# An edge layer's sum over pairs, laid out with four pair members of 32 channels in the partitions

## The chip, the cores and the metric

The kernel runs on one core of a Trainium2 chip, alone. The metric is the device time in microseconds of one execution; a lower number is better. The profile is one execution taken by the hardware profiler. It names the engines PE (TensorE matmul), PEld (TensorE weight load), DVE (VectorE), ACT (ScalarE), POOL (GpSimd) and SP (SyncE, which here only issues DMAs).

## What is computed

The reference applies four residual layers to an image batch of shape (4, 56, 56, 128): a window and global attention layer, an edge layer, a Fourier layer and a convolution. The change is in the second one:

```python
# x: (4, 56, 56, 128), after a group norm
W1, W2 = (We[:, :f], We[:, f:])
proj_i = jnp.einsum('blnf,of->blno', x, W1)
proj_j = jnp.einsum('blnf,of->blno', x, W2)
edge = jax.nn.relu(proj_i[:, :, :, None, :] + proj_j[:, :, None, :, :] + be)
edge_sum = edge.sum(axis=3)
node_in = jnp.concatenate([x, edge_sum], axis=-1)
node = jax.nn.relu(jnp.einsum('blnc,oc->blno', node_in, Wn) + bn)
```

For each image b, each line l of 56 and each channel o of 128, all 56 x 56 pairs (n, m) are formed, and their relu is summed over m. That is 4 x 56 x 56 x 56 x 128 relus, about 90 million, and no matrix product can replace them. The relu of a sum can be written without an addition: relu(a + c) = max(a, -c) + c. So an engine may take one maximum per pair, and the sum of c over those m is put in afterwards as a correction that depends on l alone.

## The kernel before

Channels lie in the 128 partitions, and an image's 3136 positions lie along the free dimension. The program is one instruction stream per engine. In `build` (L2689) four images go one after another through `first_layers`: an attention stage (`fast_layer`), then `edge_layer` (L1150), then a store of x1. The next image's attention stage starts with memsets on POOL (L339 and on), which wait until the buffers of the edge layer are released.

`edge_layer` works in seven blocks j of 8 lines (NB = 448 positions). For each block:

- `normed(j)` makes the group-normed input xg, for the first two blocks on DVE, then on ACT (L1178).
- `project(j)` (L1180) multiplies xg by W2 and W1 into two PSUM tiles, pc and pa (L1184, L1186).
- `evacuate(j)` (L1189) copies c = -(pc + be) and a = pa to SBUF on ACT (L1194, L1196), and adds the bias bn to the residual x (L1197). GpSimd works from SBUF; DVE reads a from PSUM, as pa.
- Fourteen turns take four m each, in the order of `EDGE_TURNS` (L1147). In a `d` turn DVE writes max(a, c) for four m and all 448 positions, 1792 elements per partition, into a tile e_td (L1231; seven buffers). In a `p` turn POOL writes a - c into e_tp (L1233; four buffers), and ACT takes the relu in place (L1235).
- After each turn PE adds the tile to the accumulator acc in PSUM (L1238). A turn is sixteen matmuls with a 32x32 identity: row group r is a quarter of the channels, column group q one of the four m. acc is four banks, one for each channel quarter, and the four m stay apart in its partition quarters.
- `rest` is the sum of c over the m of the `d` turns (DVE, L1248). e_sums is acc copied to SBUF (ACT, L1250).
- `output(j, rest, sums)` (L1200) adds up six matmuls of 128x128x448: xg by Wn, the correction by rest (L1203), and one for each channel quarter of the sums (L1206), whose weights Wnq sum the four m at the same time.
- `finish(j, po)` (L1209) is one DVE operation: x = max(po, -bn) + x.

The order is written out by hand for PE, ACT and DVE. At the end of block j PE does the output of block j - 1 and the projections of block j + 2; DVE does the `finish` of block j - 2 after turn 3 of block j; ACT evacuates block j + 1 after turn 5. [...] two for pc and po (tag mm), two for pa, four for acc.

After the fourth image, `build` (L2775 to L2788) loads images back from memory into a pool x2 of two buffers, s_x, for the Fourier layer. SP issues these loads in its queue as soon as the memory of the buffers is free, and then stores x1 (x2d) and loads that layer's weights (t_w_qk and others). The first matmuls of that layer read s_x (L1527).

Of the kernel before, what the change touches and what calls it, by code (L numbers as in the profile page):

```python
# [12 lines left out]
F32 = mybir.dt.float32  # L13
AF = mybir.ActivationFunctionType
ALU = mybir.AluOpType
AX = mybir.AxisListType
PSUM = bass.MemoryType.PSUM
DRAM = bass.MemoryType.DRAM

P = 128  # L20
B = 4
HH = 56
TOK = HH * HH
NB = 448
# [8 lines left out]
def bc(ap, axis, n):  # L33

    ap = ap.unsqueeze(axis)
    shape = list(ap.shape)
    shape[axis] = n
    return ap.to_broadcast(shape)


def blk(j):
    return slice(j * NB, (j + 1) * NB)
# [149 lines left out]
def apply_norm(k, out, xt, mr):  # L192
    k.nc.vector.tensor_scalar(out, xt, mr[:, 0:1], mr[:, 1:2], ALU.subtract, ALU.mult)
# [950 lines left out]

EDGE_TURNS = "ddpddpdpddpddp"  # L1147


def edge_layer(k, w, x1, st):  # L1150

    nc, tc = k.nc, k.tc
    xf = x1.rearrange("p l n -> p (l n)")
    nd = 4 * EDGE_TURNS.count("d")
    quarters = [slice(32 * q, 32 * q + 32) for q in range(4)]
    with ExitStack() as es:  # L1160
        big = es.enter_context(tc.tile_pool(name="e_big", bufs=1))
        wk = es.enter_context(tc.tile_pool(name="e_wk", bufs=2))
        psum = es.enter_context(tc.tile_pool(name="e_ps", bufs=2, space=PSUM))

        def bank():
            return psum.tile([P, 512], F32, tag="mm", name="e_mm")

        mr = group_norm_factors(k, wk, bank, st)
        xg = big.tile([P, TOK], F32, name="e_xg")
        shift = wk.tile([P, 1], F32, name="e_shift", bufs=1)  # L1170
        nc.vector.tensor_scalar(shift, mr[:, 0:1], mr[:, 1:2], -1.0, ALU.mult, ALU.mult)
        ready = {}

        def normed(j):
            if j < 2:
                apply_norm(k, xg[:, blk(j)], xf[:, blk(j)], mr)
            elif j < NBLK:
                nc.scalar.activation(xg[:, blk(j)], xf[:, blk(j)], AF.Identity, bias=shift, scale=mr[:, 1:2])  # L1178

        def project(j):  # L1180
            if j >= NBLK:
                return
            pc = psum.tile([P, 512], F32, tag="mm", name="e_pc")
            nc.tensor.matmul(pc[:, :NB], w.W2, xg[:, blk(j)], start=True, stop=True)  # L1184
            pa = psum.tile([P, 512], F32, tag="pa", name="e_pa")
            nc.tensor.matmul(pa[:, :NB], w.W1, xg[:, blk(j)], start=True, stop=True)  # L1186
            ready[j] = pa, pc

        def evacuate(j):  # L1189
            if j >= NBLK:  # L1190
                return
            pa, pc = ready[j]
            c = wk.tile([P, 8, HH], F32, name="e_c")
            nc.scalar.activation(c.rearrange("p l m -> p (l m)"), pc[:, :NB], AF.Identity, bias=w.nbe, scale=-1.0)  # L1194
            a = wk.tile([P, NB], F32, name="e_a")
            nc.scalar.copy(a, pa[:, :NB])  # L1196
            nc.scalar.activation(xf[:, blk(j)], xf[:, blk(j)], AF.Identity, bias=w.bn)  # L1197
            ready[j] = pa, a, c

        def output(j, rest, sums):  # L1200
            po = psum.tile([P, 512], F32, tag="mm", name="e_po")
            nc.tensor.matmul(po[:, :NB], w.Wn[:, 0, :], xg[:, blk(j)], start=True, stop=False)
            nc.tensor.matmul(po[:, :NB].rearrange("p (l n) -> p l n", l=8), w.nWn, bc(rest, 2, HH),  # L1203
                             start=False, stop=False)
            for r in range(4):
                nc.tensor.matmul(po[:, :NB], w.Wnq[:, r, :], sums[:, r, :], start=False, stop=(r == 3))  # L1206
            return po

        def finish(j, po):  # L1209

            nc.vector.scalar_tensor_tensor(xf[:, blk(j)], po[:, :NB], w.nbn, xf[:, blk(j)], ALU.max, ALU.add)

        with tc.manual_schedule(engines={mybir.EngineType.PE, mybir.EngineType.Activation, mybir.EngineType.DVE}):
            for j in range(2):
                normed(j)
            for j in range(2):
                project(j)
                evacuate(j)
            last = po = None
            for j in range(NBLK):  # L1220
                pa, a, c = ready.pop(j)
                acc = psum.tile([P, 4, 512], F32, name="e_acc", bufs=1)
                rest = wk.tile([P, 8], F32, name="e_rest")
                at = {"d": 0, "p": nd}
                for g, e in enumerate(EDGE_TURNS):
                    t = wk.tile([P, 4, 8, HH], F32, tag="e_" + e, name="e_t" + e, bufs=7 if e == "d" else 4)
                    cm = bc(c[:, :, at[e]:at[e] + 4].rearrange("p l m -> p m l"), 3, HH)
                    at[e] += 4
                    if e == "d":
                        am = bc(pa[:, :NB].rearrange("p (l n) -> p l n", l=8), 1, 4)  # L1230
                        nc.vector.tensor_tensor(t, am, cm, ALU.max)  # L1231
                    else:
                        nc.gpsimd.tensor_sub(t, bc(a.rearrange("p (l n) -> p l n", l=8), 1, 4), cm)  # L1233
                        tf = t.rearrange("p m l n -> p (m l n)")
                        nc.scalar.activation(tf, tf, AF.Relu)  # L1235
                    for q in range(4):
                        for r, o in enumerate(quarters):
                            nc.tensor.matmul(acc[quarters[q], r, :NB], k.ident[o, o],  # L1238
                                             t[o, q].rearrange("p l n -> p (l n)"),
                                             start=(g == 0), stop=(g == len(EDGE_TURNS) - 1))  # L1240
                    if g == 3 and po is not None:
                        finish(j - 2, po)
                    if g == 5 and j:
                        evacuate(j + 1)
                    if g == 8:
                        normed(j + 2)
                    if g == 9:
                        nc.vector.tensor_reduce(rest, c[:, :, 0:nd], AX.X, ALU.add)  # L1248
                sums = wk.tile([P, 4, NB], F32, name="e_sums")
                nc.scalar.copy(sums, acc[:, :, :NB])  # L1250
                if last:
                    po = output(*last)
                project(j + 2)
                last = j, rest, sums
            finish(NBLK - 2, po)
            finish(NBLK - 1, output(*last))


def edge_weights(k, w, pool):

    for n, t in (("nbe", w.be), ("nbn", w.bn), ("nWn", w.Wn[:, 1, :])):
        r = pool.tile(list(t.shape), F32, name="e_" + n)
        k.nc.vector.tensor_scalar_mul(r, t, -1.0)
        setattr(w, n, r)


def l1_host(i):
    We, Wn = i["L1_conv_We"], i["L1_conv_Wn"]
    W2 = Wn[:, P:].T.reshape(4, 1, 32, P)
    return {  # L1270
        "w1_W1": We[:, :P].T, "w1_W2": We[:, P:].T, "w1_be": i["L1_conv_be"].reshape(P, 1),
        "w1_Wn": Wn.T.reshape(2, P, P).transpose(1, 0, 2), "w1_bn": i["L1_conv_bn"].reshape(P, 1),
        "w1_Wnq": np.broadcast_to(W2, (4, 4, 32, P)).reshape(4, P, P).transpose(1, 0, 2),
    }


# [1388 lines left out]
def group_norm_factors(k, pool, bank, st):  # L2665

    nc = k.nc
    mv = pool.tile([P, 2], F32, tag="mv", name="gf_mv")
    nc.vector.bn_aggr(mv, st.rearrange("p a b -> p (a b)"))
    ps = bank()  # L2670
    nc.tensor.matmul(ps[:, 0:1], k.g4, mv[:, 0:1], start=True, stop=True)
    mr = pool.tile([P, 2], F32, tag="mr", name="gf_mr")
    nc.vector.tensor_copy(mr[:, 0:1], ps[:, 0:1])
    t = pool.tile([P, 1], F32, tag="gt", name="gf_t")
    nc.vector.tensor_sub(t, mv[:, 0:1], mr[:, 0:1])
    nc.vector.tensor_mul(t, t, t)
    nc.vector.tensor_add(t, t, mv[:, 1:2])
    ps = bank()
    nc.tensor.matmul(ps[:, 0:1], k.g4, t, start=True, stop=True)
    nc.scalar.activation(t, ps[:, 0:1], AF.Sqrt, bias=k.eps)  # L2680
    nc.vector.reciprocal(mr[:, 1:2], t)
    return mr
# [158 lines left out]
```

## Time and profile before

| what | us |
|---|---|
| median of three runs | 3583.2 |
| lowest and highest | 3579.53, 3584.5 |
| the profiled execution, its own time | 3579.81 |
| its span, from first to last instruction | 3578.0 |
| mean granted TensorE clock | 0.981 |
| edge layer of the first image: first e_xg to last `finish` | 549.24 to 699.71 |
| edge layer of the fourth image: the same | 2540.12 to 2690.83 |
| DVE busy with e_td (L1231), whole program | 491.2 |
| POOL busy with e_tp (L1233), whole program | 451.5 |
| PE busy with e_acc (L1238), whole program | 548.4 |

The shares on the page's first line are means over the whole program: the edge layer is about 600 of 3578 us, so a share over the program says little about what bounds it. The table by stretches is of more use: it gives each engine's busy time within a given stretch. The operations of one kind are grouped by line and shape, with the number, the busy time in all, the mean of one, and the idle time of the engine just before them with what ended it. Operations of one engine overlap a little, so the distance between two of them is less than the mean of one. The ends of matmuls are modelled, and a matmul of fp32 stands as two records.

### The profile page before, as it was taken

The page shows a single profiled execution, that of the slowest core. Times are in us where ns is not written, and L with a number is a line of the kernel's source. Part 1 is how long each engine was busy: PE and PEld are TensorE (multiplying, and loading weights), DVE is VectorE, ACT ScalarE, POOL GpSimd, SP SyncE. Part 2 cuts the span into 40 slices and gives each one's busy share as a digit, 9 for nine tenths or more (in the row PEclk, how much of TensorE's full clock was granted, in tenths as well). Part 3 has the DMA queues.
Part 4 walks back from the last instruction along what each step waited for, and adds up shares of the span by engine and source line. Part 5 has one row for each costly group of instructions (what it writes and reads, how often), then busy time and mean ns, then how long its engine had stood idle before and what let it go on. Part 6 is the DMA issues. An engine that isn't in the chain of part 4 may idle for free.

```text
span 3578.0 us, 80873 instructions
## 1 busy us (share of the span) xinstructions
PE 3372.0 (94%) x36096; PEld 1549.4 (43%) x36096; DVE 2702.3 (76%) x2531; ACT 2089.9 (58%) x2103; POOL 1249.2 (35%) x752
## 2 busy tenths in 40 slices
PE   6999998989999898999999999999898899999998
PEld 4433344553333455333344643333456443336664
DVE  6588868767888696688859758887784678886776
ACT  4688865458888564688856458887552112214442
POOL 1000017600000581000018400000673778884686
PEclk8999999999999999999999999999998999999999
DMA  2144420014333000444310024442103027763101
GB/s 103 43 92 92 95 42 20 20 47 94 88 88 83 20 3 20 99 93 94 89 44 3 20 57 94 94 94 63 38 3 101 15 53 178 181 148 91 55 19 55
DMA packets 98076, 244.51 MB, mean 68 GB/s; under 512 B 64456, under 2 KB 69832, under 8 KB 92712
## 3 DMA queue, kind: packets, MB, share of 16 engines
q0 software_dynamic: 16128, 102.77, 14.2%
q1 hardware_dynamic: 74872, 123.64, 11.9%
q10 hardware_dynamic: 6720, 12.85, 1.3%
q8 instruction: 285, 4.67, 0.5%
q14 instruction: 71, 0.58, 0.1%
HBM read 79.46 MB, written 31.33 MB: 31 GB/s over the span
## 4 chain that ended last, share of the span: by engine, by line
PE 79%; DVE 10%; ACT 4%; issue 4%; POOL 3%; DMA 0%; POOLq 0%; DVEq 0%; ACTq 0%
PE f_pm L818 17%; PE f_pm L684 15%; PE u_po L1878 8%; PE e_acc L1238 7%; PE q_acc L1732 3%; DVE e_td L1231 3%; PE f_pm L791 2%; PE e_po L1206 2%; PE f_pm L770 2%; ACT f_ring L821 1%; PE f_pm L464 1%; PE o_d L2141 1%; DVE f_acc L673 1%; PE o_d L2538 1%; PE f_pm L715 1%
## 5 line engine op out<-in xcount | busy, mean ns | idle before, releaser
L821 ACT ACTIVATE f_ring<-f_pm 128x1792 f32<-128x1792 f32 (+1 forms) x764 | 1093.8, 1482 | 228.7 <-PE f_pm L818 181.2
L673 DVE TENSOR_TENSOR f_acc<-f_acc,f_ring 128x1792 f32<-128x1792 f32 x468 | 947.7, 2025 | 191.1 <-ACT f_ring L821 160.9
L818 PE MATMUL f_pm<-f_qT,f_kT 32*128 32x448 f32 x5376 | 725.2, 571 | 15.5 <-ACT f_ring L821 5.1
L684 PE MATMUL f_pm<-f_ring,f_va 128*32 128x448 f32 (+1 forms) x6304 | 589.4, 490 | 0.0
L663 POOL DMA_DIRECT2D f_far<-f_ring x112 | 96.6, 862 | 1329.3 <-ACT f_ring L821 1108.2
L1231 DVE TENSOR_TENSOR e_td<-e_pa,e_c 128x1792 f32<-128x1792 f32 x252 | 491.2, 2018 | 14.1 <-ACT e_a L1196 14.1
L1233 POOL TENSOR_TENSOR e_tp<-e_a,e_c 128x1792 f32<-128x1792 f32 x140 | 451.5, 3261 | 101.4 <-PE e_acc L1238 59.8
L818 PEld LDWEIGHTS f_pm<-f_qT,f_kT 32*128 32x128 f32 x5376 | 260.4, 183 | 417.2 <-ACT f_ring L821 304.7
L1238 PE MATMUL e_acc<-e_td,t_shared 32*32 32x448 f32 x8064 | 325.8, 545 | 24.9 <-DVE e_td L1231 24.0
L684 PEld LDWEIGHTS f_pm<-f_ring,f_va 128*32 128x32 f32 x6304 | 164.2, 109 | 409.7 <-issue 397.4
L1873 DVE TENSOR_TENSOR u_ud<-u_px,u_d 112x1792 f32<-112x1792 f32 x144 | 263.5, 1864 | 39.6 <-PE u_po L1878 35.4
L1235 ACT ACTIVATE e_tp<-e_tp 128x1792 f32<-128x1792 f32 x140 | 233.4, 1694 | 74.0 <-POOL e_tp L1233 74.0
L1875 POOL TENSOR_TENSOR u_up<-xh,u_d 112x1792 f32<-112x1792 f32 (+1 forms) x72 | 240.9, 3376 | 55.0 <-PE u_po L1878 39.7
L1238 PE MATMUL e_acc<-e_tp,t_shared 32*32 32x448 f32 x4480 | 222.6, 544 | 3.0 <-ACT e_tp L1235 2.4
L1878 PE MATMUL u_po<-u_ud,AT 112*64 112x448 f32 x1056 | 213.8, 544 | 1.9 <-DVE u_ud L1873 1.9
L1238 PEld LDWEIGHTS e_acc<-e_td,t_shared 32*32 32x32 f32 x8064 | 142.3, 103 | 138.4 <-DVE e_td L1231 79.4
L1878 PEld LDWEIGHTS u_po<-u_ud,AT 112*64 112x64 f32 x1056 | 74.4, 138 | 128.8 <-issue 112.9
L1250 ACT COPY e_sums<-e_acc 128x1792 f32<-128x1792 f32 x28 | 46.3, 1652 | 136.2 <-PE e_acc L1238 136.2
L1238 PEld LDWEIGHTS e_acc<-e_tp,t_shared 32*32 32x32 f32 x4480 | 96.5, 103 | 53.0 <-issue 16.6
L728 DVE RECIPROCAL f_den<-f_den 128x448 f32<-128x448 f32 x28 | 82.6, 2951 | 44.1 <-ACT f_den L725 44.1
L1717 POOL TENSOR_TENSOR q_u<-iS,q_g 128x1792 f32<-128x1792 f32 x32 | 102.8, 3236 | 23.0 <-PE q_acc L1732 22.8
L1732 PE MATMUL q_acc<-q_u,S 64*64 64x448 f32 x1024 | 104.6, 553 | 4.4 <-DVE q_u L1719 3.3
(525 smaller groups left out, 4511.6 us busy)
## 6 DMA issues: line engine op xcount, KB each, us to landing
f_far<-f_ring POOLq DMA_DIRECT2D x112, 896.0 KB, 6.3
u_d<-dd SPq DMA_DIRECT2D x46, 784.0 KB
f_far<-f_ring SPq DMA_DIRECT2D x28, 896.0 KB
xw<-in_x SPq DMA_DIRECT2D x4, 1568.0 KB
x2d<-x SPq DMA_DIRECT2D x4, 1568.0 KB
xat<-x SPq DMA_DIRECT2D x4, 1568.0 KB
x_xs<-xat ACTq DMA_DIRECT2D x32, 196.0 KB
xm<-x_ev ACTq DMA_DIRECT2D x64, 98.0 KB
```

Source lines behind the costliest of these rows:

```text
L673: nc.vector.tensor_add(e.acc, e.acc, slots(j, c))
L684: nc.tensor.matmul(e.po[heads[h], part], va[o, c, heads[h]], p, start=(c == 0), stop=(c == 23 and part.stop == NB))
L818: nc.tensor.matmul(ss[:, i, :NB], kT[heads[h], c * P:(c + 1) * P], qT[heads[h], blk(j)], start=True, stop=True)
L821: nc.scalar.activation(ring[:, slot:slot + m, :], ss[:, :m, :NB], AF.Exp, scale=scale)
L1231: nc.vector.tensor_tensor(t, am, cm, ALU.max)
L1233: nc.gpsimd.tensor_sub(t, bc(a.rearrange("p (l n) -> p l n", l=8), 1, 4), cm)
L1235: nc.scalar.activation(tf, tf, AF.Relu)
L1238: nc.tensor.matmul(acc[quarters[q], r, :NB], k.ident[o, o], t[o, q].rearrange("p l n -> p (l n)"), start=(g == 0), stop=(g == len(EDGE_TUR ...
L1732: nc.tensor.matmul(acc[bp][i][halves[hb % 2], hb // 2, :NB], x[o], u[o, 8 * hb:8 * hb + 8, :].rearrange("p h t -> p (h t)"), start=first, ...
L1873: nc.vector.tensor_mul(u, bc(px[:, :, :NB], 2, m), dm)
L1875: nc.gpsimd.tensor_mul(u, bc(x, 2, m), dm)
L1878: nc.tensor.matmul(po[64 * b2:64 * b2 + 64, :NB], st.AT[:, 8 * i + h0 + q, 2 * bp + b2, :], u[:, b2, q, :], start=(left == 16), stop=(left ...
```

## The change

The layout of a turn is turned round. Before, a turn has four m in the free dimension and 128 channels in the partitions. Now a turn has four m, one from each quarter of the 56, in the four partition quarters, with 32 channels in each, and the four channel quarters r lie in the free dimension.

- `l1_host` lays W1 out so that each channel quarter r has its own 128x128 weight that repeats 32 channels four times; be is laid out the same way. `project` makes four pa tiles of 448 columns, and one pc from sixteen small matmuls (32 output partitions, 112 columns) with -W2.
- `evacuate` copies the four a to SBUF with the bias be, and c; it is split into two parts, after turns 5 and 8.
- `terms` forms a turn. On DVE the first operand is a in SBUF, the second is pc in PSUM; on POOL it is a and c in SBUF.
- A turn of PE is four matmuls with 128 rows and 32 output partitions. The weight S sums the four m. acc is one bank, and its four quarters are the channel quarters, so the sums are 128x448 instead of 128x1792.
- The correction by rest is added into acc with -S, and `output` has two matmuls instead of six.
- Of fourteen turns eight are `d`, five `p`, and one `s`, half on DVE and half on POOL (before: nine and five). e_td has six buffers, and the half tiles have two buffers each. The banks of PSUM: one for po, four for pa, two for pc, one for acc.
- In block 0 the first three `d` turns and the first `p` turn are made quarter by quarter, as the a tiles arrive.

```diff
-EDGE_TURNS = "ddpddpdpddpddp"
+EDGE_TURNS = "ddpddpsdpdpddp"
...
-            pc = psum.tile([P, 512], F32, tag="mm", name="e_pc")
-            nc.tensor.matmul(pc[:, :NB], w.W2, xg[:, blk(j)], start=True, stop=True)
-            pa = psum.tile([P, 512], F32, tag="pa", name="e_pa")
-            nc.tensor.matmul(pa[:, :NB], w.W1, xg[:, blk(j)], start=True, stop=True)
+            pa = [psum.tile([P, 512], F32, name="e_pa", bufs=4) for r in range(4)]
+            pc = psum.tile([P, 512], F32, name="e_pc", bufs=2)
+
+            def first(r):
+                nc.tensor.matmul(pa[r][:, :NB], w.W1[:, r, :], xg[:, blk(j)], start=True, stop=True)
+            first(0)
+            xm = xg[:, blk(j)].rearrange("p (l m) -> p l m", l=8)
+            for r, o in enumerate(quarters):
+                for q in range(4):
+                    nc.tensor.matmul(pc[quarters[q], 8 * M * r:8 * M * (r + 1)].rearrange("p (l m) -> p l m", l=8),
+                                     w.nW2[:, o], xm[:, :, M * q:M * (q + 1)], start=True, stop=True)
+            for r in range(1, 4):
+                first(r)
...
+            for r in range(2 * part, 2 * part + 2):
+                nc.scalar.activation(a[:, r, :], pa[r][:, :NB], AF.Identity, bias=w.be[:, r:r + 1])
+                if r == 0:
+                    nc.scalar.copy(c.rearrange("p r l m -> p (r l m)"), pc[:, :NB])
+            if part == 1:
+                nc.scalar.activation(xf[:, blk(j)], xf[:, blk(j)], AF.Identity, bias=w.bn)
+
+        def terms(j, m, t, r0, r1, e):
+
+            pc, _, c, a = ready[j]
+            if e == "d":
+                c = pc[:, :NB].rearrange("p (r l m) -> p r l m", r=4, l=8)
+            cm = bc(c[:, r0:r1, :, m], 3, HH)
+            am = a[:, r0:r1, :].rearrange("p r (l n) -> p r l n", l=8)
+            if e == "d":
+                nc.vector.tensor_tensor(t, am, cm, ALU.max)
+            else:
+                nc.gpsimd.tensor_sub(t, am, cm)
+                tf = t.rearrange("p r l n -> p (r l n)")
+                nc.scalar.activation(tf, tf, AF.Relu)
...
-            nc.tensor.matmul(po[:, :NB].rearrange("p (l n) -> p l n", l=8), w.nWn, bc(rest, 2, HH),
-                             start=False, stop=False)
-            for r in range(4):
-                nc.tensor.matmul(po[:, :NB], w.Wnq[:, r, :], sums[:, r, :], start=False, stop=(r == 3))
+            nc.tensor.matmul(po[:, :NB], w.Wn[:, 1, :], sums, start=False, stop=True)
...
-                acc = psum.tile([P, 4, 512], F32, name="e_acc", bufs=1)
-                rest = wk.tile([P, 8], F32, name="e_rest")
-                at = {"d": 0, "p": nd}
+                acc = psum.tile([P, 512], F32, name="e_acc")
+                rest = wk.tile([P, 4, 8], F32, name="e_rest")
+                at, ms = {"d": 0, "p": nd + ns, "s": nd}, []
...
-                    for q in range(4):
-                        for r, o in enumerate(quarters):
-                            nc.tensor.matmul(acc[quarters[q], r, :NB], k.ident[o, o],
-                                             t[o, q].rearrange("p l n -> p (l n)"),
-                                             start=(g == 0), stop=(g == len(EDGE_TURNS) - 1))
+                    elif e == "s":
+                        parts = [(tile_of("d", 2), 0), (tile_of("p", 2), 2)]
+                        for t, r in parts:
+                            terms(j, m, t, r, r + 2, "p" if r else "d")
+                    else:
+                        parts = [(tile_of(e), 0)]
+                        terms(j, m, parts[0][0], 0, 4, e)
+                    for t, r0 in parts:
+                        for r in range(t.shape[1]):
+                            nc.tensor.matmul(acc[quarters[r0 + r], :NB], w.S[:, 0, :], t[:, r].rearrange("p l n -> p (l n)"),
+                                             start=(g == 0), stop=False)
...
-                sums = wk.tile([P, 4, NB], F32, name="e_sums")
-                nc.scalar.copy(sums, acc[:, :, :NB])
+                for r in range(4):
+                    nc.tensor.matmul(acc[quarters[r], :NB].rearrange("p (l n) -> p l n", l=8), w.S[:, 1, :],
+                                     bc(rest[:, r, :], 2, HH), start=False, stop=True)
+                sums = wk.tile([P, NB], F32, name="e_sums")
+                nc.scalar.copy(sums, acc[:, :NB])
```

More of the change, by code (lines that the diff above doesn't have):

```diff
@@ L1157, in edge_layer @@
     xf = x1.rearrange("p l n -> p (l n)")
-    nd = 4 * EDGE_TURNS.count("d")
+    M = HH // 4
+    nd, ns = EDGE_TURNS.count("d"), EDGE_TURNS.count("s")
     quarters = [slice(32 * q, 32 * q + 32) for q in range(4)]
@@ L1162, in edge_layer @@
         wk = es.enter_context(tc.tile_pool(name="e_wk", bufs=2))
-        psum = es.enter_context(tc.tile_pool(name="e_ps", bufs=2, space=PSUM))
+        psum = es.enter_context(tc.tile_pool(name="e_ps", bufs=1, space=PSUM))
         def bank():
@@ L1182, in project @@
                 return
-            pc = psum.tile([P, 512], F32, tag="mm", name="e_pc")
-            nc.tensor.matmul(pc[:, :NB], w.W2, xg[:, blk(j)], start=True, stop=True)
-            pa = psum.tile([P, 512], F32, tag="pa", name="e_pa")
-            nc.tensor.matmul(pa[:, :NB], w.W1, xg[:, blk(j)], start=True, stop=True)
-            ready[j] = pa, pc
-        def evacuate(j):
+            pa = [psum.tile([P, 512], F32, name="e_pa", bufs=4) for r in range(4)]
+            pc = psum.tile([P, 512], F32, name="e_pc", bufs=2)
@@ L1190, in evacuate @@
+            for r in range(1, 4):
+                first(r)
+            c = wk.tile([P, 4, 8, M], F32, name="e_c")
+            a = wk.tile([P, 4, NB], F32, name="e_a")
+            ready[j] = pc, pa, c, a
+        def evacuate(j, part):
             if j >= NBLK:
                 return
[L1192 to L1200, printed above, removed]
+            pc, pa, c, a = ready[j]
+            for r in range(2 * part, 2 * part + 2):
+                nc.scalar.activation(a[:, r, :], pa[r][:, :NB], AF.Identity, bias=w.be[:, r:r + 1])
+                if r == 0:
+                    nc.scalar.copy(c.rearrange("p r l m -> p (r l m)"), pc[:, :NB])
@@ L1201, in output, with tile_of @@
+        def tile_of(e, n=4):
+            return wk.tile([P, n, 8, HH], F32, tag="e_%s%d" % (e, n), name="e_t" + e,
+                           bufs=2 if n < 4 else 6 if e == "d" else 4)
+        def output(j, sums):
             po = psum.tile([P, 512], F32, tag="mm", name="e_po")
             nc.tensor.matmul(po[:, :NB], w.Wn[:, 0, :], xg[:, blk(j)], start=True, stop=False)
-            nc.tensor.matmul(po[:, :NB].rearrange("p (l n) -> p l n", l=8), w.nWn, bc(rest, 2, HH),
-                             start=False, stop=False)
@@ L1215, in edge_layer @@
                 normed(j)
-            for j in range(2):
-                project(j)
-                evacuate(j)
+            project(0)
+            for part in range(2):
+                evacuate(0, part)
+            project(1)
             last = po = None
             for j in range(NBLK):
-                pa, a, c = ready.pop(j)
-                acc = psum.tile([P, 4, 512], F32, name="e_acc", bufs=1)
-                rest = wk.tile([P, 8], F32, name="e_rest")
-                at = {"d": 0, "p": nd}
-                for g, e in enumerate(EDGE_TURNS):
[L1226 to L1231, printed above, removed]
-                    else:
-                        nc.gpsimd.tensor_sub(t, bc(a.rearrange("p (l n) -> p l n", l=8), 1, 4), cm)
-                        tf = t.rearrange("p m l n -> p (m l n)")
-                        nc.scalar.activation(tf, tf, AF.Relu)
-                    for q in range(4):
-                        for r, o in enumerate(quarters):
-                            nc.tensor.matmul(acc[quarters[q], r, :NB], k.ident[o, o],
-                                             t[o, q].rearrange("p l n -> p (l n)"),
-                                             start=(g == 0), stop=(g == len(EDGE_TURNS) - 1))
@@ new lines, in edge_layer @@
+                acc = psum.tile([P, 512], F32, name="e_acc")
+                rest = wk.tile([P, 4, 8], F32, name="e_rest")
+                at, ms = {"d": 0, "p": nd + ns, "s": nd}, []
+                for e in EDGE_TURNS:
+                    ms.append(at[e])
+                    at[e] += 1
+                early = {}
+                if j == 0:
+                    early = {g: tile_of(EDGE_TURNS[g]) for g in
+                             [g for g, e in enumerate(EDGE_TURNS) if e == "d"][:3] + [EDGE_TURNS.index("p")]}
+                    for r in range(4):
+                        for g, t in early.items():
+                            terms(j, ms[g], t[:, r:r + 1], r, r + 1, EDGE_TURNS[g])
@@ new lines, in edge_layer @@
+                for g, e in enumerate(EDGE_TURNS):
+                    m = ms[g]
+                    if g in early:
+                        parts = [(early[g], 0)]
+                    elif e == "s":
+                        parts = [(tile_of("d", 2), 0), (tile_of("p", 2), 2)]
+                        for t, r in parts:
+                            terms(j, m, t, r, r + 2, "p" if r else "d")
+                    else:
+                        parts = [(tile_of(e), 0)]
[4 more added lines that the diff above has]
+                                             start=(g == 0), stop=False)
@@ L1241, in edge_layer @@
                     if g == 3 and po is not None:
                         finish(j - 2, po)
-                    if g == 5 and j:
-                        evacuate(j + 1)
+                    if g == 5:
+                        evacuate(j + 1, 0)
                     if g == 8:
+                        evacuate(j + 1, 1)
+                    if g == 10:
                         normed(j + 2)
-                    if g == 9:
-                        nc.vector.tensor_reduce(rest, c[:, :, 0:nd], AX.X, ALU.add)
@@ L1249, in edge_layer @@
-                sums = wk.tile([P, 4, NB], F32, name="e_sums")
-                nc.scalar.copy(sums, acc[:, :, :NB])
+                    if g == 8:
+                        if ns:
+                            nc.vector.tensor_reduce(rest[:, 0:2], ready[j][2][:, 0:2, :, 0:nd + 1], AX.X, ALU.add)
+                        nc.vector.tensor_reduce(rest[:, 2 if ns else 0:4], ready[j][2][:, 2 if ns else 0:4, :, 0:nd], AX.X, ALU.add)
+                for r in range(4):
+                    nc.tensor.matmul(acc[quarters[r], :NB].rearrange("p (l n) -> p l n", l=8), w.S[:, 1, :],
+                                     bc(rest[:, r, :], 2, HH), start=False, stop=True)
@@ L1253, in edge_layer @@
                 project(j + 2)
-                last = j, rest, sums
+                last = j, sums
             finish(NBLK - 2, po)
@@ L1259, in edge_weights @@
 def edge_weights(k, w, pool):
-    for n, t in (("nbe", w.be), ("nbn", w.bn), ("nWn", w.Wn[:, 1, :])):
+    for n, t in (("nW2", w.W2), ("nbn", w.bn)):
         r = pool.tile(list(t.shape), F32, name="e_" + n)
@@ L1268, in l1_host @@
     We, Wn = i["L1_conv_We"], i["L1_conv_Wn"]
-    W2 = Wn[:, P:].T.reshape(4, 1, 32, P)
+    W1 = np.broadcast_to(We[:, :P].T.reshape(P, 4, 1, 32), (P, 4, 4, 32)).reshape(P, 4, P)
+    S = np.tile(np.eye(32, dtype=np.float32), (4, 1))
     return {
-        "w1_W1": We[:, :P].T, "w1_W2": We[:, P:].T, "w1_be": i["L1_conv_be"].reshape(P, 1),
+        "w1_W1": W1, "w1_W2": We[:, P:].T, "w1_be": np.tile(i["L1_conv_be"].reshape(4, 32).T, (4, 1)),
         "w1_Wn": Wn.T.reshape(2, P, P).transpose(1, 0, 2), "w1_bn": i["L1_conv_bn"].reshape(P, 1),
-        "w1_Wnq": np.broadcast_to(W2, (4, 4, 32, P)).reshape(4, P, P).transpose(1, 0, 2),
+        "w1_S": np.stack((S, -S), 1),
     }
```

## The prediction

> **What bounds the kernel now.** I read the page's first part, then the edge layer by stretches of one block, then the chain of waits there, the groups by shape, and the layer's two ends.
>
> ```profile
> PE 3372.0 (94%) x36096; PEld 1549.4 (43%) x36096; DVE 2702.3 (76%) x2531; ACT 2089.9 (58%) x2103; POOL 1249.2 (35%) x752
> ```
>
> These are averages over unlike stages. The edge layer runs four times (once per image), seven blocks each. Two of its blocks in the table by stretches (columns: stretch, length, then PE, weight loads, DVE, ACT, POOL busy, clock, DMA):
>
> ```profile
> 617.30:636.98 19.68, 19.68 (x475) 11.71 (x480) 18.42 (x12) 12.09 (x10) 16.14 (x5) 1.00 0.01 2
> 636.98:656.67 19.69, 19.69 (x476) 11.71 (x483) 18.43 (x12) 12.09 (x10) 16.13 (x5) 1.00 0.01 3
> ```
>
> The period is 19.68 us and PE is busy for all of it; DVE has 1.26 us to spare, POOL 3.55, ACT 7.6. The chain of waits has PE alone:
>
> ```profile
> 612.79 3.01 PE e_po L1206 x8
> 615.80 0.75 PE e_pc L1184 x2
> 616.55 0.75 PE e_pa L1186 x2
> 617.30 13.47 PE e_acc L1238 x436
> 630.77 0.95 PE e_po L1202 x2
> 631.72 0.75 PE e_po L1203 x2
> 632.48 3.01 PE e_po L1206 x8
> ```
>
> So 13.47 us are the fourteen turns, 4.71 the output product, 1.50 the next block's projections. Every fp32 matmul is recorded as two passes of 0.375 us at 448 columns (3.01/8). A turn takes 13.47/14 = 0.96 us: 32 passes of 32x32, one each 30 ns. Sixteen tiles at once would need 2 x 0.375 = 0.75, so they are limited by their number. The groups of those three blocks by shape:
>
> ```profile
> L1231 DVE TENSOR_TENSOR e_td<-e_pa,e_c 128x1792 f32<-128x1792 f32 x28 | 54.7, 2018 | 0.0
> L1233 POOL TENSOR_TENSOR e_tp<-e_a,e_c 128x1792 f32<-128x1792 f32 x16 | 51.7, 3258 | 9.1 <-PE e_acc L1238 9.1
> L1235 ACT ACTIVATE e_tp<-e_tp 128x1792 f32<-128x1792 f32 x15 | 25.1, 1691 | 4.5 <-POOL e_tp L1233 4.5
> L1211 DVE SCALAR_TENSOR_TENSOR x<-e_po,e_nbn,x 128x448 f32<-128x448 f32 x3 | 2.1, 685 | 3.8 <-PE e_po L1206 3.8
> ```
>
> DVE and POOL both wait for PE, at `finish` (3.8/3 = 1.26) and for a free e_tp buffer. Back to back the operations overlap: five e_td take 9.74 us in the timeline, so one costs (9.74 - 2.02)/4 = 1.93; fourteen e_tp take 45.07, so one costs 3.22. At the layer's end:
>
> ```profile
> 689.74 1.65 ACT L1250 COPY e_sums<-e_acc 128x1792 f32<-128x1792 f32 x1 [6.75 <-PE e_acc L1238]
> 699.03 0.68 DVE L1211 SCALAR_TENSOR_TENSOR x<-e_po,e_nbn,x 128x448 f32<-128x448 f32 x1 [3.89 <-PE e_po L1206]
> 699.13 0.12 POOL L339 MEMSET w_xg<- 128x16 f32 x1 [17.86 <-PE e_po L1206]
> ```
>
> The next image begins on POOL, with memsets that wait for the last e_po matmul. Every microsecond by which that matmul comes earlier is gained.
>
> [...] a stretch with nothing but L684 (128 rows, 32 columns, 448 wide):
>
> ```profile
> 323.77:325.41 1.64, 1.64 (x16) 0.42 (x16) 1.00 0.19 35
> ```
>
> 16 passes at four abreast need 16 x 0.375/4 = 1.50; the other 0.14 is about what a switch costs. [...] Here DVE had a in PSUM and c in SBUF and now has the reverse: one of each[...].
>
> **The change, per block.**
> PE: turns 14 x 4 matmuls x 2 passes at four abreast = 14 x 0.75 = 10.5. The correction by rest, moved into acc, 0.75. Output 2 matmuls = 4 x 0.375 = 1.5 (was 4.7). Four first projections 8 x 0.375 = 3.0. The second projection is 16 matmuls of 112 columns, 32 passes; by columns 0.75, by number 32 x 0.0325 = 1.04 (L405's 32 passes of 66 columns fill 1.04 us), taken. Four mode switches x 0.15 = 0.6. Sum 17.4.
> DVE: 8 x 1.93 = 15.4; the half turn 0.99 (u_ud 112x896: 1.08, less the overlap of 0.09); two reductions of 144 and 128 elements in place of one of 288 (0.45): 0.2 each; `finish` 0.6. Sum 17.4. That c as second operand in PSUM is as fast: f_oT<-f_oT,f_pm at 128x448, 896, 1344 has 0.612, 1.080, 1.548, a line that gives 2.016 at 1792, the 2.018 of e_td. A stride-0 innermost read from PSUM is not in the trace: below, no DVE TENSOR_TENSOR row lies under that line, so no gain; above, POOL's kind of slowdown, kept as a rival.
> POOL: 5 x 3.22 = 16.1 plus half a turn. Nearest: y<-y,q_den 128x896 at 1.69 (a broadcast operand, as here) and o_o 128x896 at 2.08 (none); I take 1.69, 1.65 after overlap. Sum 17.75 (to 18.15).
> ACT: relus 5 x 1.6 + 0.9, four a's at 0.6, c 0.5, x 0.6, xg 0.7, sums 0.5 (was 1.65): 13.6.
> So POOL sets the period at about 17.75, PE and DVE 0.35 behind. Do the waits let it? Let POOL end a block at 0. Its last relu ends at 1.7, PE's turn and rest at 3.25, output 4.9, projections 9.3, the next turns at the earliest 19.8; the next last relu comes at 19.45. ACT waits for acc until 3.25, then relu, a0, c, a1 (8 to 10), a2, a3 (13 to 15): before POOL needs them at 17.75. The e_tp buffer that POOL needs at 14.5 is free at 11.6; DVE's six e_td buffers let it run ahead, and `finish` finds its po at 5. No wait stops POOL. Gain 19.68 - 17.75 = 1.93 per block.
>
> **The ends.** Start: e_xg is ready at 549.8 as before. PE is at half clock there (e_pc 0.82 per pass): first(0) 1.65, second projection about 1.6, c copied 0.5, so POOL starts near 553.95 (was 553.74) on quarter pieces of about 0.95 (4 x 0.95 against 3.22) and ends block 0 at 553.95 + 3.8 + 4 x 3.22 + 1.65 = 572.3, block 6 at 572.3 + 6 x 17.75 = 678.8. Then relu 1.7, turn 0.75, rest 0.75, switch and output(5) 1.65, `finish` 0.9 (e_mm now has one buffer, so output(6) waits for it), output(6) 1.5: 686.1, against 698.95. Per image -12.9, four images -51.5.
>
> **A cost elsewhere.** The edge pool grew: in the built programs it ended at byte 189088 of a partition and now at 196192, while the first s_x buffer of the next stage lies at 191040 in both. Before:
>
> ```profile
> 2531.47 2.07 SPq L2781 DMA_DIRECT2D s_x<-xad x4
> 2691.04 6.22 PE L1527 MATMUL s_pr<-t_images,s_x 128*64 128x33 f32 x207 [1.00 <-PE e_po L1206]
> ```
>
> The loads were issued before the fourth image's edge layer; 3.2 MB took 2533 to 2541, about 400 GB/s. Now they overlap e_sums and wait for the last e_po. PE starts L1527 with the first half of image 0: the bytes began to flow some 2 us after the issue, and 0.8 MB at 400 GB/s take 2, so 3 us later than before, and again a little for the second half. Queued behind on SP: x2d and all weights; t_w_qk, which came before them, lands some 16 us later, and POOL's score weights end 5 us later, at about 2743 less the gain, far ahead of their use at 2784. The 3.24 us that PE stood at 2697 with all DMA engines busy may come again or be covered. Bounds 0 and 8; I take +3.5, once. The edge pack loads 61 columns fewer and one small DVE op goes: nothing.
>
> Sum: -51.5 + 3.5 = -48. The profiled execution (span 3578.0, time 3579.8) becomes 3531.8; the median of runs, 3583.2, stands 3.4 above it, so 3535.
>
> **Rivals.**
> Likeliest, POOL-bound: 3535, its own range 3526 to 3546. For: three engines' sums within 0.35 us, the longest decides; POOL was never short of work by more than buffers.
> PE stays the bound, or three nearly equal engines in strict order lose 0.6 a block to one another: 18.35, 28 x 0.6 = 17 us less gain: 3552. For: switches and small matmuls are the least certain terms. Against: L684 and L405 show both.
> More gain: s_x hidden, starts as before: 3527.
> Slower: POOL's op in the new layout[...] slows to u_up's 4.01 (POOL's longest at this size). Price: 5.5 x 0.79 = 4.35 us per block, 28 x 4.35 = 122, so 3657. It decides from 48/(28 x 5.5) = 0.31 us more per op, that is from 3.53. Against: a and c are read as before, one plain and one broadcast innermost. The same mechanism on DVE would need 1.93 to become about 2.3.
>
> **How the numbers follow.** Likeliest 0.60, PE or mutual stalls 0.20, more gain 0.08, slower 0.10, all gains given back 0.02. A measurement tells 0.2% (7 us) from no change. Range 3522 to 3561: it takes in the first three cases but for a tail and leaves out about 0.15. Faster 0.88, same 0.02, slower 0.10.
>
> **What would show it.** Period 17.7 to 17.9 with POOL without gaps and PE waiting for e_tp: right. PE full at 18 or more: the second case. e_td over 2.1 or e_tp over 3.4: the slower one. e_acc passes near 94 ns a piece; L1527's successor 3 to 4 us late after e_po. Wrong if POOL waits for a or c from ACT, or if DVE cannot run ahead of `finish`.

## The result, and the profile after

The changed kernel takes 3542.99 us, the median of four runs (3540.41 to 3546.04), against 3581.77 us (3579.53 to 3584.5) in the runs of the kernel before beside it: a ratio of 0.9892, 95% interval 0.9875 to 0.9909. The profiled executions have spans of 3538.6 and 3578.0 us, so the traces differ by 39.4 us. 48 were forecast.

First the edge layer over one block (stretch, length, then busy time of PE, weight loads, DVE, ACT and POOL, clock, DMA share, GB/s), in the changed kernel:

```profile
602.99:620.77 17.78, 17.62 (x168) 6.46 (x164) 17.52 (x13) 13.36 (x15) 17.78 (x7) 1.00 0.01 2
```

POOL is busy for the whole of the period, 17.78 us, and DVE and PE for all but a quarter of a microsecond and less. The groups by shape, over three such blocks:

```profile
L1224 POOL TENSOR_TENSOR e_tp<-e_a,e_c 128x1792 f32<-128x1792 f32 x16 | 51.7, 3259 | 0.0
L1222 DVE TENSOR_TENSOR e_td<-e_a,e_pc 128x1792 f32<-128x1792 f32 x25 | 49.1, 2014 | 0.0
L1224 POOL TENSOR_TENSOR e_tp<-e_a,e_c 128x896 f32<-128x896 f32 x3 | 5.2, 1722 | 0.0
L1195 PE MATMUL e_pc<-e_xg,e_nW 128*32 128x112 f32 x96 | 2.9, 261 | 0.0
L1240 DVE SCALAR_TENSOR_TENSOR x<-e_po,e_nbn,x 128x448 f32<-128x448 f32 x3 | 2.1, 684 | 0.8 <-PE e_po L1235 0.8
```

The operations cost what they cost before: e_tp 3.259 us (3.258), e_td 2.014 (2.018), with c read from PSUM. What has gone is the idle time in front of them: 9.1 us of POOL's waiting for PE is 0.0. Only `finish` still waits, 0.26 us a block.

From the first e_xg to the start of the last `finish`, the four edge layers take 149.79, 149.80, 150.66 and 150.03 us before, and 138.44, 137.56, 137.39 and 137.97 after: 48.9 us less in all.

The seam behind the fourth image, where the edge layer ends and the Fourier layer begins, gives part of it back. From the last `finish` to the first q_acc matmul of the Fourier layer it is 97.1 us before (2690.15 to 2787.28) and 105.0 after (2640.34 to 2745.31), 7.8 more. The two s_pt matmuls of the image norm, L1499 and L1508 in the changed kernel, divide this stretch in three. Its front, from the last `finish` to the first of them, takes 29.4 us before and 33.1 after. From the first to the second it is 9.8 and 14.0 us, and from there to q_acc 58.0 and 57.9. So 3.7 us are lost in the front and 4.3 in the middle. The timeline of the changed kernel there (start, length, engine, line, what, count, and in brackets the idle time before and what ended it):

```profile
2639.39 0.91 PE L1235 MATMUL e_po<-e_sums,t_edge 128*128 128x448 f32 x2
2640.44 2.06 SPq L2827 DMA_DIRECT2D s_x<-xad  x4
2645.79 8.45 PE L1573 MATMUL s_pr<-t_images,s_x 128*64 128x33 f32 x209 [5.49 <-DMA s_x<-xad]
2657.27 1.93 SPq L158 DMA_DIRECT2D t_w_qk<-in_w_qk  x2
2673.40 0.38 PE L1499 MATMUL s_pt<-s_mv,t_shared 128*128 128x1 f32 x2 [2.67 <-DVE s_mv L1496]
2677.11 2.68 DVE L1504 TENSOR_TENSOR s_t<-s_mv,s_mr 128x1 f32<-128x1 f32 x1
2679.82 7.56 DVE L1505 SCALAR_TENSOR_TENSOR s_t<-s_t,s_mv 128x1 f32<-128x1 f32 x1
2686.74 1.39 POOL L1667 TENSOR_SCALAR d_t<-t_w_V,t_images 128x448 f32<-128x448 f32 x1
2687.43 0.59 PE L1508 MATMUL s_pt<-s_t,t_shared 128*128 128x1 f32 x2 [9.39 <-DVE s_t L1505]
```

And the same places of the kernel before that have not been shown:

```profile
2690.21 0.81 SPq L158 DMA_DIRECT2D t_w_qk<-in_w_qk  x2
2719.55 0.38 PE L1453 MATMUL s_pt<-s_mv,t_shared 128*128 128x1 f32 x2 [2.67 <-DVE s_mv L1450]
2723.54 5.46 DVE L1458 TENSOR_TENSOR s_t<-s_mv,s_mr 128x1 f32<-128x1 f32 x1
2728.36 1.39 POOL L1621 TENSOR_SCALAR d_t<-t_w_V,t_images 128x448 f32<-128x448 f32 x1
2729.31 0.58 PE L1462 MATMUL s_pt<-s_t,t_shared 128*128 128x1 f32 x2 [4.78 <-DVE s_t L1459]
```

Two things are to be seen. In the front PE stands 5.49 us for the s_x loads, where it stood 1.00. Part of that comes back: PE's second stop among the same matmuls, 3.24 us before, is 0.98 after. And in the middle two operations of one element per partition (s_t) take 10.2 us together where they took 5.7, and PE waits for them 9.39 us instead of 4.78. In both kernels the stalled s_t ends 0.64 us after POOL begins the same operation, d_t (2686.74 to 2687.38, and 2728.36 to 2729.00). POOL comes to d_t 46.4 us after the end of the last e_po, 8.1 later than before (38.3). Its weights come late: the load of t_w_qk is issued 17 us after the last e_po instead of at once, and that of t_w_qkr follows behind it.

The rest is small: the attention stages of the four images are 0.9 us shorter in the trace after, and 2.6 us go near the end, where the same piece of the last layer ran at a lower clock. By stretches, after and before:

```profile
3484.00:3499.00 15.00, 12.15 (x36) 6.18 (x36) 10.58 (x16) 2.91 (x4) 13.20 (x8) 0.77 0.00 0
```

```profile
3525.00:3540.00 15.00, 12.15 (x43) 6.11 (x43) 11.29 (x17) 2.96 (x4) 13.98 (x9) 1.00 0.00 0
```

So -48.9 - 0.9 + 7.8 + 2.6 = -39.4. The mean clock of this piece was 0.77 in the one execution and 1.00 in the other, and medians of single kernels here have intervals of about 0.15% (5 us) to either side. What is a few microseconds is therefore read below from distances within the traces: the edge layer's length, and that from last `finish` to first q_acc.

### The profile page after: what moved, and what is told of

Same layout as the page of the kernel before. It is cut to its first block, busy times and chain, and to the rows that moved or that the text cites. A ratio compares the mean times of both kernels' runs of the same rounds, so it can differ in the third digit from the quotient of the medians.

```text
span 3538.6 us, 64314 instructions
## 1 busy us (share of the span) xinstructions
PE 3314.0 (94%) x27696; PEld 1425.9 (40%) x27696; DVE 2684.4 (76%) x2594; ACT 2128.8 (60%) x2227; POOL 1297.8 (37%) x792
## 4 chain that ended last, share of the span: by engine, by line
PE 72%; POOL 9%; DVE 8%; issue 5%; ACT 5%; DMA 0%; POOLq 0%; DVEq 0%; ACTq 0%
PE f_pm L818 18%; PE f_pm L684 15%; PE u_po L1924 8%; POOL e_tp L1224 7%; PE q_acc L1778 3%; PE f_pm L791 2%; PE e_acc L1277 2%; PE f_pm L770 2%; ACT f_ring L821 1%; PE o_d L2584 1%; PE f_pm L464 1%; PE e_pa L1190 1%; PE o_d L2187 1%; DVE f_acc L673 1%; PE s_pr L1573 1%
## 5 line engine op out<-in xcount | busy, mean ns | idle before, releaser
L684 PE MATMUL f_pm<-f_ring,f_va 128*32 128x448 f32 (+1 forms) x6304 | 590.1, 491 | 0.0
L1224 POOL TENSOR_TENSOR e_tp<-e_a,e_c 128x1792 f32<-128x1792 f32 (+2 forms) x180 | 499.9, 2819 | 43.9 <-issue 42.6
L1222 DVE TENSOR_TENSOR e_td<-e_a,e_pc 128x1792 f32<-128x1792 f32 (+2 forms) x288 | 467.1, 1690 | 15.1 <-ACT e_c L1210 14.9
L684 PEld LDWEIGHTS f_pm<-f_ring,f_va 128*32 128x32 f32 x6304 | 163.8, 109 | 410.8 <-issue 398.4
L1226 ACT ACTIVATE e_tp<-e_tp 128x1792 f32<-128x1792 f32 (+1 forms) x180 | 263.3, 1484 | 94.1 <-POOL e_tp L1224 94.1
L1277 PE MATMUL e_acc<-e_td,t_edge 128*32 128x448 f32 x1904 | 218.9, 541 | 0.0
L1277 PE MATMUL e_acc<-e_tp,t_edge 128*32 128x448 f32 x1232 | 154.9, 545 | 36.1 <-ACT e_tp L1226 33.3
L1277 PEld LDWEIGHTS e_acc<-e_td,t_edge 128*32 128x32 f32 x1904 | 63.1, 110 | 126.5 <-issue 112.4
L1763 POOL TENSOR_TENSOR q_u<-iS,q_g 128x1792 f32<-128x1792 f32 x32 | 102.8, 3235 | 22.8 <-PE q_acc L1778 22.8
L804 POOL TENSOR_TENSOR x<-xf,xw 128x343 f32<-128x343 f32 x28 | 25.5, 910 | 225.7 <-DVE xf L793 225.7
L2022 ACT COPY x_ev<-x_po 56x896 f32<-56x896 f32 x32 | 28.8, 900 | 128.9 <-DMA x_xs<-xat 51.6
```

The source lines that it names most:

```text
L684: nc.tensor.matmul(e.po[heads[h], part], va[o, c, heads[h]], p, start=(c == 0), stop=(c == 23 and part.stop == NB))
L1224: nc.gpsimd.tensor_sub(t, am, cm)
L1277: nc.tensor.matmul(acc[quarters[r0 + r], :NB], w.S[:, 0, :], t[:, r].rearrange("p l n -> p (l n)"), start=(g == 0), stop=False)
```

## Experiments

**Which engine sets the period.** Two other splits of the fourteen turns, and one kernel with less work for PE.

```diff
-EDGE_TURNS = "ddpddpsdpdpddp"
+EDGE_TURNS = "ddpddpddpdpddp"
```

> The changed kernel with nine turns for VectorE, five for GpSimd and none shared, the split of the kernel before (no half tiles, so the pool ends below s_x as well, which the first edit alone showed to give 2.8 us). Theory (the longest of three engines sets the period): VectorE 9 x 1.93 + 0.36 + 0.60 = 18.3, GpSimd 16.1, TensorE 17.6: period 18.4 (18.3 to 18.6), that is 17 us more over 28 blocks: 3557 us. Rival (TensorE or a chain of waits at 17.8 sets it): period 17.8, 3540.

Measured 3543.5 us, ratio to the kernel before 0.9900 (0.9883 to 0.9916). The period is 18.33, by the start of successive `finish`; by stretches:

```profile
602.00:620.33 18.33, 17.43 (x168) 6.51 (x164) 18.33 (x12) 12.32 (x14) 16.15 (x6) 1.00 0.01 2
```

DVE is the full one now, as worked out. The time was missed by 14 us for two reasons that the traces give. The layer grows by only 1.7 us an image (139.5 on average against 137.8), since of its six distances between one `finish` and the next only the first four are 18.33: at the layer's end, with POOL ahead, the fifth is 16.87, against 17.77 in the changed kernel; and the seam takes 98.9 instead of 105.0. Together +6.7 - 6.1.

```diff
-EDGE_TURNS = "ddpddpsdpdpddp"
+EDGE_TURNS = "ddpddppdpdpddp"
```

> The changed kernel with eight turns for VectorE, six for GpSimd and none shared. Theory: GpSimd 6 x 3.22 = 19.3 us a block, 1.55 x 28 = 43 us more: 3583 us. Rival (GpSimd isn't the bound): period 17.8, 3540.

Measured 3583.7 us, ratio 1.0004 (0.9995 to 1.0013): the whole gain is gone. By stretches:

```profile
602.00:621.32 19.32, 17.64 (x166) 6.45 (x165) 16.45 (x10) 14.29 (x15) 19.32 (x7) 1.00 0.01 1
```

```diff
-                for r in range(4):
-                    nc.tensor.matmul(acc[quarters[r], :NB]..., w.S[:, 1, :], bc(rest[:, r, :], 2, HH), ...)
```

> The changed kernel without the correction by rest on TensorE (eight matmul records a block; the sum over the VectorE terms is left without its c). Theory (GpSimd sets the period, TensorE's 17.6 us beside it are cover): period stays 17.78, only the 0.75 us at each image's end go: 3540 us. Rival (TensorE at 17.6 us sets it and GpSimd follows through the e_tp buffers): period 17.0 to 17.1, 20 us less: 3522.

Measured 3538.4 us, ratio 0.9876 (0.9860 to 0.9893), with the edge layers 1.06 us shorter on average. By stretches:

```profile
602.00:619.78 17.78, 16.88 (x157) 6.18 (x156) 17.52 (x13) 13.38 (x14) 17.78 (x7) 1.00 0.00 1
```

PE has 0.74 us less to do in each block and the period doesn't move. This kernel leaves the correction out of its sums, so it serves for its time alone. The three together settle it: the period is that of the longer of POOL and DVE, and PE at 17.62 is cover, if only just.

**What the start in pieces is worth.**

```diff
-                if j == 0:
+                if j < 0:
                     early = {g: tile_of(EDGE_TURNS[g]) for g in
```

> The changed kernel without the quarter pieces: in block 0 every turn is one operation, which waits for all four a. Theory (GpSimd sets the period, so nothing that starts it later is caught up): its first whole e_tp starts at about 556.9 in the first image and ends at 560.2, against 558.2 with the pieces; 2.0 us per image, 8 in all: 3551 us. Rival (TensorE sets the period and has the tiles of VectorE to work on meanwhile): less than 1 us per image, 3543 to 3547.

Measured 3553.0 us, ratio 0.9916 (0.9902 to 0.9930). In this kernel POOL's first operation stands in the timeline as

```profile
556.05 19.50 POOL L1224 TENSOR_TENSOR e_tp<-e_a,e_c 128x1792 f32<-128x1792 f32 x7 [13.05 <-issue]
```

where the changed kernel's first piece starts at 553.52. The four edge layers take 139.50, 139.61, 139.47 and 140.85, 8.1 us more than with the pieces: 2.0 an image. With POOL as the bound, what it starts late it ends late.

**What it is worth that DVE's second operand lies in PSUM.**

```diff
-            if e == "d":
-                c = pc[:, :NB].rearrange("p (r l m) -> p r l m", r=4, l=8)
```

> The changed kernel in which VectorE takes c from the copy in SBUF too, so that both its operands lie in SBUF beside a GpSimd that works all the time. Theory (a VectorE operation with two SBUF operands and a GpSimd operation exclude each other): per block 8 x 1.93 + 0.99 of VectorE and 17.75 of GpSimd can't overlap, a period of up to 34 us, 16 x 28 = 450 us longer: about 3990 us, e_td or e_tp far over 2.0 and 3.26 in the profile. Rival (there is no such exclusion, the second operand's place is free): period 17.8, 3543.

Measured 3981.8 us, in one run. The period alternates between 33.9 and 33.3 us. Groups by shape over about two blocks:

```profile
L1220 DVE TENSOR_TENSOR e_td<-e_a,e_c 128x1792 f32<-128x1792 f32 x16 | 62.7, 3969 | 0.0
L1222 POOL TENSOR_TENSOR e_tp<-e_a,e_c 128x1792 f32<-128x1792 f32 x9 | 42.7, 4756 | 12.7 <-PE e_acc L1275 12.7
```

The same operations, with both of DVE's tensors in SBUF, go from 2.014 to 3.969 and from 3.259 to 4.756 us on average. By the durations that they have in the changed kernel, the turns of a block are 16.4 us of work for DVE and 17.75 for POOL, 34.2 one after the other, and the period is 33.6: nearly as long as if each stood while the other runs. One operand's place costs 439 us here.

**The seam, taken apart.** First the loads: one buffer for each kind of half tile, so that the pool ends below s_x as in the kernel before.

```diff
-                           bufs=2 if n < 4 else 6 if e == "d" else 4)
+                           bufs=1 if n < 4 else 6 if e == "d" else 4)
```

> The changed kernel with one buffer instead of two for each kind of half tile; the edge pool ends at byte 189024 again, below the first s_x buffer at 191040. Theory (the seam cost about 8 us, in two pieces): the s_x loads are issued ahead of the fourth image's edge layer, the first s_pr matmul starts 1.0 us after the last e_po matmul (5.5 in the changed kernel), and t_w_qk is loaded ahead of t_w_ms, so that GpSimd's score weights run earlier and VectorE's two one-element operations s_t take about 5.7 us together instead of 10.2. That is -4.5 and -4: 3535 us against 3543. Rival 1 (only the wait for s_x is real, the long s_t a chance): 3539. Rival 2 (all of it is hidden, the missing gain is in the clock): 3543.

Measured 3539.7 us, ratio 0.9873 (0.9858 to 0.9888); the seam takes 102.2 us instead of 105.0. The loads are issued at 2499.88, before the fourth edge layer. In its timeline:

```profile
2649.67 4.10 PE L1573 MATMUL s_pr<-t_images,s_x 128*64 128x33 f32 x81 [2.91 <-DMA t_w_qk<-in_w_qk]
2656.32 7.32 PE L1573 MATMUL s_pr<-t_images,s_x 128*64 128x33 f32 x143 [2.55 <-issue]
2688.44 2.21 DVE L1504 TENSOR_TENSOR s_t<-s_mv,s_mr 128x1 f32<-128x1 f32 x1
2690.68 0.23 DVE L1505 SCALAR_TENSOR_TENSOR s_t<-s_t,s_mv 128x1 f32<-128x1 f32 x1
2690.97 0.59 PE L1508 MATMUL s_pt<-s_t,t_shared 128*128 128x1 f32 x2 [1.55 <-DVE s_t L1505]
```

The stall of s_t goes from 10.2 us to 2.4, and PE's wait for it from 9.39 to 1.55, more than expected. POOL now comes to d_t 39.7 us after the last e_po, near the 38.3 of the kernel before, so the late loads are what made it late. But only 2.8 us of the 7.8 come back, for the front of the seam got longer: 37.3 us from the last `finish` to the first s_pt, against 33.1 in the changed kernel. Part of the shorter stall is due to that, since DVE itself comes to s_t 4.9 us later. PE still stands 2.91 us before s_pr, where 1.0 was expected, and then 224 of its matmuls take 11.4 us of busy time, 51 ns each, where before 207 took 6.22, 30 ns each. That is the clock: it is 0.50 in this run's stretch from 2650.80 to 2652.80, with 43 matmuls. By stretches, two of the changed kernel and two of the kernel before:

```profile
2644.34:2646.34 2.00, 0.55 (x11) 0.58 (x12) 0.00 (x0) 0.00 (x0) 0.00 (x0) 0.50 1.01 416
2646.34:2648.34 2.00, 2.00 (x42) 2.00 (x42) 0.00 (x0) 0.00 (x0) 0.00 (x0) 0.50 1.04 381
```

```profile
2692.15:2694.15 2.00, 2.00 (x76) 2.00 (x73) 0.31 (x1) 0.00 (x0) 1.08 (x5) 1.00 0.74 247
2702.15:2704.15 2.00, 1.83 (x4) 1.26 (x5) 2.00 (x18) 0.98 (x3) 0.00 (x0) 0.50 0.19 44
```

Around the wait of 5.49 us PE had half the clock, 42 matmuls in 2 us instead of 76, and it had the whole clock again some 4.8 us after it began s_pr (0.50 up to 2650.50, 1.00 from 2650.75). In this run it had 0.50 behind the waits of 2.91 us (2650.80 to 2652.80) and 2.55 us (2658.80 to 2672.80) too. So these waits are paid for twice, once standing and once in the matmuls behind them. The kernel before pays as well, at 0.50 behind its stop of 3.24 us, as the last line shows. By the clock of such stretches, the front of the seam has some 7 us at half clock before, some 10 in the changed kernel, and some 20 in this run.

Next the stall of s_t by itself: the two operations take and leave their difference in PSUM, so that none has two tensors in SBUF.

```diff
-    nc.vector.tensor_sub(t1, mv[:, 0:1], mr[:, 0:1])
-    nc.vector.scalar_tensor_tensor(t1, t1, t1, mv[:, 1:2], ALU.mult, ALU.add)
+    tp = ps[:, 2:3]
+    nc.vector.tensor_sub(tp, mv[:, 0:1], ps[:, 0:1])
+    nc.vector.scalar_tensor_tensor(t1, tp, tp, mv[:, 1:2], ALU.mult, ALU.add)
```

> The changed kernel in which the two one-element operations s_t of the image norm take their difference from and through PSUM, so that neither has two operands in SBUF. Theory (VectorE with two SBUF operands and GpSimd exclude each other, and s_t waits until GpSimd reaches an operation that lets go): s_t falls to about 0.2 us each, TensorE's wait of 9.4 us before the second s_pt falls below 2 us, and the time by 5 to 8 us: 3535 to 3538. Rival 1 (s_t is held up by something else, such as a semaphore the profile doesn't show): s_t stays at 10 us together and the time at 3543. Rival 2 (the wait only moves to the next operation with two SBUF operands, s_d): TensorE's wait goes on there, 3541 to 3543.

Measured 3539.6 us, ratio 0.9879 (0.9864 to 0.9894), between what was expected and what its second rival gave; the seam takes 102.3. Its timeline:

```profile
2676.87 0.15 DVE L1505 TENSOR_TENSOR s_pt<-s_mv,s_pt 128x1 f32<-128x1 f32 x1
2681.09 3.58 DVE L1518 TENSOR_TENSOR s_d<-s_d 128x56 f32<-128x56 f32 x1
2684.60 3.73 DVE L1519 TENSOR_TENSOR s_sq<-s_rows 128x56 f32<-128x56 f32 x1
2692.10 0.68 PE L1533 MATMUL s_pt<-s_mean,c_ones_c 128*128 128x56 f32 x2 [11.67 <-DVE s_mean L1529]
```

The operation that took 2.68 us takes 0.15, at the same place beside the same POOL, so the second operand's place is the cause of its length. But most of the wait moves to the next operations with two tensors in SBUF (s_d and s_sq, 3.58 and 3.73 us; in the changed kernel 0.20 and 0.25): it was that rival's mechanism that took over, with 2.7 us gained all the same. The kernel without the correction shows the same by another way: POOL is as late there (d_t 46.2 us after the last e_po), s_t happens to stand for only 0.60 us, and the seam still takes 102.8.

> Both edits together. Theory: the loads' 4.5 us and s_t's whole stall, up to 8.8 us in the changed kernel, go: 3530 to 3534 us. If the two losses are one and the same (the late loads), it gives no more than the first edit alone, 3535. If neither counts: 3543.

Measured 3540.2 us, ratio 0.9886 (0.9871 to 0.9901), not the 3530 to 3534 expected; the seam takes 99.05. By this distance the two losses are two: 2.8 and 2.7 alone, 5.9 together. The medians of these three kernels don't tell them apart.

**A better version.** At the end of each image PE waits 0.78 us for `finish` to release the only bank of po. The last block's po may take a bank of e_pc instead. The first kernel has this and s_t through PSUM, the second the single half tiles as well.

```diff
-            po = psum.tile([P, 512], F32, tag="mm", name="e_po")
+            po = psum.tile([P, 512], F32, tag="e_pc", name="e_po", bufs=2) if j == NBLK - 1 else psum.tile([P, 512], F32, tag="mm", name="e_po")
```

> The second edit (s_t through PSUM) and the last block's po in a bank of e_pc, which is free by then, in place of the one bank that `finish` of the block before has to release. TensorE no longer stands 0.8 us at each image's end: 137.0 us from first e_xg to last `finish` where the changed kernel has 137.8 on average, 3 us in all, and 2.7 us at the seam as before: 3537 us. Rival: the 0.8 us is made up for by `finish` and the next image's start anyway: 3540.

Measured 3537.1 us, ratio 0.9865 (0.9850 to 0.9880); the edge layers take 136.8 us on average instead of 137.8.

> All three edits. 3 us from the image ends and 5.9 us from the seam (the distance from the last `finish` to the first q_acc matmul was 99.05 with both seam edits, 104.97 in the changed kernel): 3534 us. Rival: what the medians of the single edits showed, no more than either alone: 3537 to 3540.

Measured 3528.4 us, ratio 0.9843 (0.9830 to 0.9857), which is faster than both kernels; the edge layers take 136.9 and the seam 97.4. It is more than was expected: the seam is 1.7 us shorter than with the same two edits alone, and why was not found. In its timeline:

```profile
2635.85 0.92 PE L1235 MATMUL e_po<-e_sums,t_edge 128*128 128x448 f32 x2
2639.31 4.55 PE L1574 MATMUL s_pr<-t_images,s_x 128*64 128x33 f32 x81 [2.54 <-DMA t_w_qk<-in_w_qk]
```

**What stays open.** In all kernels with early loads the first s_pr comes 2.5 to 3.1 us after the last e_po, in step with the landing of t_w_qk, which it doesn't read.

> The kernel before once more, for one thing: how long TensorE stands between the last e_po and the first s_pr. If 1.0 us is what that kernel does, it will be 1.0 again, and the 2.8 to 3.1 us of the kernels with early loads have a cause of their own. If it is chance, it will be nearer 3.

It was 1.00 us again (2691.91 for s_pr, seam 97.0 us). So this wait belongs to the changed kernels, and which of their differences makes it was not found.

## Why the prediction was right, and where it was short

**Turns and period: right.** PE was forecast at 17.4 us a block and has 17.62, DVE at 17.4 and has 17.52, POOL at 17.75 and has 17.78, ACT at 13.6 and has 13.36. Four passes of 32 columns abreast, and about 0.15 us for a switch to another shape of matmul, were estimates from the stretch of L684. In the changed kernel the eight passes of one e_acc turn follow those of the last every 0.75 us (602.72, 603.47, 604.22), which is 8 x 0.375/4; where the shape changes it takes 0.12 us more from e_rest to e_po (610.80 to 611.67), 0.09 from e_pa to e_pc (613.28 to 614.12) and 0.20 from the last e_pa to e_acc (615.03 to 617.48, against 6 x 0.375). POOL without gaps is what the forecast named as the sign for its likeliest case, and the other two splits move the period to the number worked out from the same durations (18.33 and 19.32). The case of mutual stalls at 18.35 didn't come.

**c as second operand in PSUM: right.** 2.014 us for 2.016 on the line through three other shapes. That DVE and POOL would leave each other alone with one of DVE's tensors in PSUM, whichever it is, was the author's assumption; e_tp took 3.258 us before, beside a DVE busy for 18.42 of 19.68 us, and 3.259 after, for 17.52 of 17.78; with both of DVE's tensors in SBUF it took 4.756. The half turn on POOL took 1.72 where 1.69 was taken, the second projection 0.90 of TensorE's time where 1.04 was. The slower rival, a longer e_tp or e_td, had no part.

**Waits: right.** POOL never waits for a, c or a buffer after the start, DVE only 0.26 us for `finish`.

**The ends: right in kind, 2.6 us short over four images.** In the first image POOL starts at 553.52 (553.95 forecast), but its second piece waits 0.86 us for the second a; it ends block 6 at 679.37 (678.8), and the last `finish` begins at 687.15, where 686.1 was given for the e_po matmul before it. Saved are 12.2 us an image on average, not 12.9.

**The cost elsewhere: the term that was short.** 3.5 us were taken, between bounds of 0 and 8, and 7.8 measured. The 3.5 stood for the wait for s_x, and the front of the seam did lose 3.7. That the two agree is in part luck, for the pieces do not: PE stood 4.5 us longer before s_pr where 3 had been taken, its second stop, which the prediction left open, shrank from 3.24 to 0.98 us, and some 3 us more at half clock stood in no term. The other 4.3 us had been set at nothing, and this is the step that failed. The prediction saw that t_w_qk would come some 16 us later and that POOL's score weights would end 5 us later (POOL came to d_t 8.1 later), and called that free since they are used long after. Their use is not what counts: while POOL works on them back to back, DVE's norm operations with two SBUF tensors stand (s_t 2.68 and 7.56 us), and PE behind them (9.39). What the edge layer shows only in the run with c in SBUF was at work in the next stage, in the kernel before too (5.46 us), and the change moved more of POOL's work onto it.

**The rest** of the distance to the forecast, 2.6 us, is the clock near the end of this one execution. So 48 less 2.6, less 4.3, less 2.6, plus 0.9 from the attention stages is the 39.4 of the traces; the medians say 38.8.

## What to carry to other kernels

When several engines share a sum, add up each engine's block from measured durations: here such sums gave the period of three splits within 0.1 us, and only work taken off the longest engine moved it. Where DVE and POOL work side by side, count the SBUF tensors among DVE's inputs before anything else; here one of the two in PSUM was worth a factor of nearly two in the period (17.78 against 33.6 us). And when a pool grows, ask which later loads lose their early start, what their queue then holds back, and which engine will be disturbed by work that has become late though nobody waits for its result.

## What the runs showed of the hardware that was not expected

A VectorE operation of one element per partition stood for 7.56 us beside GpSimd. It did not wait for one GpSimd operation alone: eleven of them, of 0.24 to 1.25 us each, ran one after another while it stood. In four kernels (the one before, the changed one, the one without pieces and the first other split) a standing s_t ended 0.63 to 0.64 us after the same operation, a TENSOR_SCALAR with one tensor (d_t), had begun. Why it ended there was not found. With long operations on both sides, as with c in SBUF, both kept going, one e_td in 3.97 us and one e_tp in 4.76 on average.

TensorE's clock fell to half around waits of only 2.91 and 2.55 us in the first kernel with early loads, and around the second it stayed there for some 17 us; in the changed kernel, around the wait of 5.49 us, for some 7.
